# Products on GpSimd and more additions on TensorE in the last three units of an involution, shared out by a tally

## The chip, the cores and the metric

The kernel runs on one core of a Trainium2 chip. The metric is the device time in microseconds, the median of several runs. Engines are named as in the profile: PE is TensorE (PEld its weight loads), DVE is VectorE, ACT is ScalarE, POOL is GpSimd, SP issues most DMAs. A time such as "2567 us" is counted from the start of the profiled span.

## What is computed

The input `x` has 4 images of 512 channels and 64 x 64 pixels, in float32. Layer 0 is a self-attention over the 4096 pixels of each image (queries, keys and values of 128 channels), projected back to 512 channels and added to `x`. Layer 1 is a bottleneck around an involution. The change is in the involution:

```
out = relu(affine(conv1x1(x, W1), s1, b1))            # 128 channels
w = relu(affine(conv1x1(out, Wr), sr, br))            # 32 channels
w = conv1x1(w, Ws) + bs                               # 8 groups x 49 taps, for each pixel
patches = [out shifted by (i, j) for i in 7 for j in 7]
out = sum over the 49 taps of w[group, tap] * patches # 16 channels share a group's weight
x = affine(conv1x1(out, W3), s3, b3) + x
```

For each pixel and channel there are 49 products and 48 additions, and the weight of a product is one value for 16 channels.

## The kernel before

**The two jobs.** Attention goes image by image (b = 0 to 3) and within an image by chunks of 512 pixels (c = 0 to 7). It keeps TensorE busy nearly all the time. The involution of an image runs beside the attention of later chunks and the next image, on VectorE and GpSimd. It is cut into units `u` of four image rows, 16 to an image; a unit holds its pixels on the partitions (two rows of 64) and two such tiles (`NT = 2`), with the 128 channels along the free axis. `ring` is an SBUF ring of image rows, already shifted for the seven columns, which `pump` (lines 257 to 285) fills by DMA from a copy `pix` in DRAM.

**A unit** (`involution`, lines 313 to 410). `weights` (line 290) lets TensorE make all 49 x 8 weights of each pixel into a PSUM tile `pw` of 392 columns for each of the two tiles. Then come 14 to 21 steps `o` over the seven columns `x` and groups of taps `dy`, each with a product (line 371) `ring * pw` on VectorE. It covers n taps and two tiles: 1024 columns for n = 4, 768 for 3, 512 for 2, 256 for 1. The first group at x = 0 is written to `acc` directly; the others go to one of four buffers `prod` and are added to `acc` by GpSimd (line 399). When a unit has finished, its four partial sums are folded, turned so that channels lie on the partitions (`turn_unit`), and multiplied by `W3` (`close_chunk`, which makes `py` on TensorE, and `x` on VectorE at line 485, and then the store).

**The last stretch.** When the attention of the last image has been issued, `tail` becomes true (it is set behind the last call of `attention`). What is then left are the last units of image 3: unit 13, unit 14, and unit 15, the last. (Unit 12 has its products behind it there.) In the tail every second product is added by TensorE: a transposing matmul against the identity, 128 x 128 in each piece, accumulates it into the PSUM tile `pa` (line 227), which also turns it. The others go on to `acc` through GpSimd, and `add_sums` adds `acc` to `pa` at the unit's end. The rule is one line:

```python
elif tail and (o % 2 or ending and o >= len(ops) - 4):
```

`ending` means unit 15, where the order of steps also changes, so that its later taps come in pieces of 256 columns.

**Order.** Before the tail, counters (`pe`, `due`, and `free` for each engine, advanced by `takes` and `pe_us`) decide when a step is issued. In the tail nothing waits on them: the generators `finishing`, `closing` and `taps` are stepped in turn, and the tile framework and its scheduler put each engine's instructions in an order that is fixed when the program is built. Each engine takes its queue strictly in that order, and a wait at its head holds all behind it.

Of the kernel before, what the change touches and what calls it, by code (L numbers as in the profile page):

```python
# [8 lines left out]
F32 = mybir.dt.float32  # L9
# [6 lines left out]
P = 128  # L16
CT = C // P
CH = 512
# [7 lines left out]
NTAP = K * K  # L26
GC = 16
G = P // GC
# [23 lines left out]
NT = UR // 2  # L52
# [8 lines left out]
DYS = (0, 4), (4, 3)  # L61
# [12 lines left out]
HOP_US = 0.8  # L74
STEP_US = 1.0
POOL_LAG = 4.0, 7.5
PIECE = 3
TB = 32
WARM = 8
# [7 lines left out]
def fast_path(  # L87
# [20 lines left out]
    nc = tc.nc  # L108

    def pool(name, bufs, **kw):  # L110
        return ctx.enter_context(tc.tile_pool(name=name, bufs=bufs, **kw))

    const = pool("const", 1)
    xpool = pool("x", 6)
# [46 lines left out]
    pe = 0.0  # L161
    due, seen = 0.0, 0.0
    free = {"dve": 0.0, "pool": 0.0, "dma": 0.0}
    tail = []
    reds, sums_c = {}, {}
    written = {}
    landing = {}
# [7 lines left out]
    def pe_us(us):  # L175
        nonlocal pe
        pe += us

    def takes(engine, us):
        free[engine] = max(free[engine], pe) + us  # L180
# [44 lines left out]
    def turned_add(o, lhsT, start, stop):  # L225
        pe_us(0.11)
        nc.tensor.matmul(o, lhsT=lhsT, rhs=ident, start=start, stop=stop, is_transpose=True)
# [51 lines left out]
        pace()  # L279


    def weights(b, u):
        red, col = reds[b, u]
        wpools.append(wpools.pop(0))
        pw = wpools[0].tile([P, NT, CH], F32, tag="w", name=f"pw_{b}_{u}")
        for t in range(NT):

            rows = slice(t * (P // NT), t * (P // NT) + CR + 1)
            pixels = slice(col, col + P)
            mm(  # L290
                pw[:, t, : NTAP * G], red[rows, pixels], wt[rows, O_WT : O_WT + NTAP * G],
                shared=2,
            )
        return pw
# [18 lines left out]
    def involution():  # L313
        nonlocal low, due
        while True:
            while not units:
                yield "none"
            b, u = units.pop(0)
            acc = work2.tile([P, NT, 4, P], F32, tag="acc", name=f"acc_{b}_{u}")
            yield from until(free["dve"] + 0.3)  # L320
            pw = early.pop((b, u), None) or weights(b, u)
            begin = pe + 0.5
            pa, ops = None, []
            base = b * STEP + u * UR
            for dy0, n in DYS:

                at = (base + dy0) % RING
                whole = at + n + NT < RING + 1
                pieces = [(dy0, n)] if whole else [(dy0, 2), (dy0 + 2, n - 2)]
                ops += [((0, 1), x, dy, k) for x in range(K) for dy, k in pieces]  # L330
            ending = (b, u) == (B - 1, NU - 1)
            if ending:

                ops = [op for op in ops if op[2] < DYS[1][0]]
                for x in range(K):
                    ops += [((0, 1), x, 4, 1), ((0,), x, 5, 2)]
            for o, (tiles, x, dy, n) in enumerate(ops):
                if o and dy >= DYS[1][0] > ops[o - 1][2]:
                    low = base + UR
                    pump()  # L340
                    if tail and units:
                        early[units[0]] = weights(*units[0])
                rows = [(base + dy + t * 2) % RING for t in range(NT)]
                while base + dy + n + 2 * tiles[-1] > load:
                    yield "wait"
                landed = max(landing[base + dy + 2 * t + i] for t in tiles for i in range(n))
                while not tail and (
                    pe < max(begin, landed)
                    or free["dve"] > pe + (4.5 if b == B - 1 else 3.5)
                    or free["pool"] > pe + lag  # L350
                ):
                    yield "wait"
                cost = n * len(tiles) / NT
                free["pool"] = max(free["pool"], takes("dve", DVE_TAPS[0] + DVE_TAPS[1] * cost))
                takes("pool", POOL_TAPS[0] + POOL_TAPS[1] * cost)
                due -= cost
                d0 = dy - DYS[dy >= DYS[1][0]][0]
                first = x == 0 and dy < DYS[1][0]
                prod, p0 = acc, d0
                if not first:  # L360
                    prod, p0 = prods.tile(
                        [P, NT, 4, P], F32, tag="prod", name=f"prod_{b}_{u}_{o}"
                    ), 0
                nt = len(tiles)
                col = (x * K + dy) * G
                lines = ring[:, rows[0] : rows[0] + n, x, :]
                image = bass.AP(
                    tensor=lines.tensor, offset=lines.offset,
                    ap=[lines.ap[0], [(rows[1] - rows[0]) * K * P, nt], [K * P, n], [1, P]],
                )  # L370
                product = nc.vector.tensor_tensor(  # L371
                    prod[:, :nt, p0 : p0 + n, :].rearrange("p t d (g c) -> p t d g c", g=G),
                    image.rearrange("p t d (g c) -> p t d g c", g=G),
                    pw[:, :nt, col : col + n * G].unsqueeze(3)
                    .broadcast_to([P, nt, n * G, GC])
                    .rearrange("p t (d g) c -> p t d g c", d=n),
                    ALU.mult,
                )
                if not tail:
                    tc.keep_in_program_order(product)  # L380
                if first:
                    pass
                elif tail and (o % 2 or ending and o >= len(ops) - 4):

                    begun = pa is not None
                    if not begun:
                        pa = ps1.tile([P, NT, P], F32, tag=("po", "acc")[u % 2], name=f"pa_{b}_{u}")
                    closes = ending and o == len(ops) - 1
                    if closes:
                        add_sums(pa, acc, False)  # L390
                    for t in tiles:
                        for d in range(n):
                            turned_add(
                                pa[:, t, :], prod[:, t, d, :],
                                not begun and t == d == 0,
                                closes and t == tiles[-1] and d == n - 1,
                            )
                else:
                    nc.gpsimd.tensor_tensor(  # L399
                        acc[:, :nt, d0 : d0 + n, :], acc[:, :nt, d0 : d0 + n, :],  # L400
                        prod[:, :nt, :n, :], ALU.add,
                    )
                yield
            low = max(low, (b + 1) * STEP if u == NU - 1 else base + UR)
            pump()
            if pa is None:
                for n in (2, 1):
                    nc.gpsimd.tensor_tensor(  # L408
                        acc[:, :, :n, :], acc[:, :, :n, :], acc[:, :, n : 2 * n, :], ALU.add
                    )  # L410
            closing.append(turn_unit(b, u, acc, pa, takes("pool", POOL_OP * 1.5)))


    def add_sums(pa, acc, closes):
        for t in range(NT):
            for d in range(4):
                turned_add(
                    pa[:, t, :], acc[:, t, d, :], False, closes and t == NT - 1 and d == 3
                )
# [58 lines left out]
    def close_chunk(b, c, off, n, acc):  # L478
        xt = xs[b, c][:, :, off : off + n]
        yield  # L480
        for t in range(CT):
            py = ps.tile([P, CH], F32, tag="mm", name=f"py_{b}_{c}_{off}_{t}")[:, :n]
            mm(py, w_slice(O_W3, t), acc[:, off : off + n])
            takes("dve", DVE_OP * n / CH)
            nc.vector.scalar_tensor_tensor(  # L485
                xt[:, t, :], py, v1(V_S3 + t), xt[:, t, :], ALU.mult, ALU.add
            )
            if n < CH:
                nc.sync.dma_start(out_r[b, :, t, c * CH + off : c * CH + off + n], xt[:, t, :])
            for _ in range(2):  # L490
                yield
        takes("dma", X_US)
        if n == CH:
            nc.sync.dma_start(out_r[b, :, :, c * CH + off : c * CH + off + n], xt)
# [249 lines left out]
    for b in range(B):  # L744
        lag = POOL_LAG[0]
        kv = keys_values(b)
        lag = POOL_LAG[1]
        if b == 0:
# [22 lines left out]
            )  # L771
        attention(b, *kv)
    tail.append(True)
    scorepool.close()
    wpools.insert(0, pool("ps_w", 1, space=bass.MemoryType.PSUM, reuse_waits="tile"))
    wpools.reverse()
# [404 lines left out]
```

## Time and profile before

| what | us |
|---|---|
| median of 3 runs | 2601.13 (2601.11 to 2601.95) |
| the profiled execution, its own time | 2602.08 |
| its span, first to last instruction | 2600.3 |
| TensorE busy in the span | 2576.0 (99%) |
| VectorE, GpSimd, ScalarE busy in the span | 1873.2, 1828.4, 835.5 |
| chain that ended last, PE's share of the span | 89% |
| last score matmul of the attention starts | about 2530 |
| last `x` of the involution ends on VectorE | 2594.34 |

The profile's page describes one execution. For most of the span the chain that ended last runs on TensorE, in the attention. The last 70 us are different, since there is no attention left to fill TensorE with: this is the stretch that the change touches. A group row shows line, engine, operation, output and inputs with their shapes, the count, then busy time and the mean of one instruction, then the idle time of the engine ahead of it and what ended that. A chain row shows when a piece begins and how long it holds the end. The clock in the tables of stretches is the share of full speed that TensorE was granted.

### The profile page before, as it was taken

Reading aid. Unit: us, or ns where it says so; the run is one execution under the profiler, and the core shown is the slowest. Engines: PE = TensorE matmul, PEld = TensorE weight load, DVE = VectorE, ACT = ScalarE, POOL = GpSimd, SP = SyncE. Lnnn points to the kernel's source line nnn. Section 1 sums busy time; section 2 is a strip of 40 time slices with the busy share of each in tenths; the row PEclk is TensorE's granted clock in tenths of the full one; section 3 lists DMA queues with packets and bytes.
Section 4 is the critical chain, followed back from the end, with each engine's and each line's share of the span. In section 5 each row is a group of like instructions: output and inputs, shape, how many; then the busy total and the mean of one; then the engine's idle time right before and its main releaser. Section 6 shows DMA issues by size and latency. Waiting matters only on the chain.

```text
span 2600.3 us, 24194 instructions
## 1 busy us (share of the span) xinstructions
PE 2576.0 (99%) x7290; PEld 1226.7 (47%) x7290; DVE 1873.2 (72%) x2686; ACT 835.5 (32%) x1379; POOL 1828.4 (70%) x1204
## 2 busy tenths in 40 slices
PE   9999999999999999999999999999999999999997
PEld 7444444445544444444654444444464444444574
DVE  0347778877585787788676677787856677778887
ACT  1333333332233333333223333333323333333330
POOL 0006788877881788888885468887878577778986
PEclk9999999999999999999999999999999999999998
DMA  6033233445615343333651434434463432223343
GB/s 237 1 74 64 56 81 78 99 99 150 164 43 113 63 101 88 67 81 81 181 134 44 104 69 101 97 83 86 102 178 82 113 94 70 71 63 73 65 112 83
DMA packets 208472, 243.34 MB, mean 94 GB/s; under 512 B 109576, under 2 KB 128464, under 8 KB 208208
## 3 DMA queue, kind: packets, MB, share of 16 engines
q1 hardware_dynamic: 207904, 241.39, 38.5%
q8 instruction: 58, 0.95, 0.2%
q14 instruction: 78, 0.64, 0.1%
q10 hardware_dynamic: 432, 0.36, 0.1%
HBM read 192.65 MB, written 49.06 MB: 93 GB/s over the span
## 4 chain that ended last, share of the span: by engine, by line
PE 89%; POOL 5%; DVE 4%; issue 2%; ACT 0%; DVEq 0%; POOLq 0%; ACTq 0%
PE pss L223 31%; PE po L223 30%; POOL acc L399 4%; PE pv L223 4%; PE pk L223 4%; PE pq L223 4%; PE pwo L223 4%; PE p L223 4%; PE py L223 4%; DVE prod L371 2%; PE pw L223 2%; DVE pacc L734 1%; PE pr L223 1%; POOL acc L408 0%; DVE x L485 0%
## 5 line engine op out<-in xcount | busy, mean ns | idle before, releaser
L399 POOL TENSOR_TENSOR acc<-acc,prod 128x768 f32<-128x768 f32 (+3 forms) x1068 | 1704.5, 1614 | 748.8 <-DVE prod L371 704.2
L223 PE MATMUL pss<-q,k 128*128 128x512 f32 (+1 forms) x2112 | 1056.7, 585 | 0.0
L223 PE MATMUL po<-pt,v 128*128 128x512 f32 (+1 forms) x2112 | 1048.0, 581 | 0.0
L703 ACT ACTIVATE pt<-pss 128x512 f32<-128x512 f32 x1024 | 611.0, 597 | 1244.4 <-PE pss L223 1174.7
L371 DVE TENSOR_TENSOR prod<-ring,pw 128x512 f32<-128x512 f32 (+3 forms) x1099 | 887.0, 843 | 47.1 <-POOL acc L399 43.4
L734 DVE TENSOR_TENSOR pacc<-pacc,pt 128x512 f32<-128x512 f32 x958 | 665.8, 695 | 238.2 <-ACT pt L703 210.2
L223 PEld LDWEIGHTS po<-pt,v 128*128 128x128 f32 x2112 | 399.1, 190 | 481.4 <-issue 460.9
L223 PEld LDWEIGHTS pss<-q,k 128*128 128x128 f32 x2112 | 391.8, 190 | 467.2 <-issue 462.0
L431 DVE STREAM_TRANSPOSE turned<-acc 128x256 f32<-128x256 f32 x48 | 21.4, 445 | 216.0 <-POOL acc L408 216.0
L223 PE MATMUL py<-accT,wt 128*128 128x512 f32 (+1 forms) x264 | 133.8, 590 | 4.6 <-DVE x L485 3.4
L223 PE MATMUL pwo<-on,wt 128*128 128x512 f32 (+1 forms) x264 | 128.5, 579 | 0.0
L408 POOL TENSOR_TENSOR acc<-acc 128x512 f32<-128x512 f32 x122 | 121.4, 995 | 9.6
L223 PEld LDWEIGHTS pv<-wt,x 128*128 128x128 f32 x1024 | 119.6, 192 | 15.3 <-issue 15.3
L485 DVE SCALAR_TENSOR_TENSOR x<-py,vec,x 128x512 f32<-128x512 f32 (+1 forms) x132 | 96.0, 727 | 38.3 <-PE py L223 38.1
L223 PE MATMUL pv<-wt,x 128*128 128x128 f32 x1024 | 120.2, 275 | 0.0
L223 PE MATMUL p<-x,wt 128*128 128x512 f32 (+1 forms) x264 | 119.3, 580 | 0.0
L223 PE MATMUL pk<-x,wt 128*128 128x512 f32 x256 | 118.0, 600 | 0.0
L614 ACT ACTIVATE x<-x,vec 128x512 f32<-128x512 f32 (+1 forms) x132 | 92.9, 707 | 74.9 <-PE p L223 58.2
L223 PE MATMUL pq<-x,wt 128*128 128x512 f32 (+1 forms) x264 | 115.3, 579 | 0.0
L587 DVE SCALAR_TENSOR_TENSOR x<-pwo,bo,x 128x512 f32<-128x512 f32 (+1 forms) x132 | 95.3, 729 | 21.2 <-PE pwo L223 19.9
L371 DVE TENSOR_TENSOR acc<-ring,pw 128x1024 f32<-128x1024 f32 (+1 forms) x84 | 78.7, 956 | 15.6 <-PE pw L223 15.6
L223 PEld LDWEIGHTS pq<-x,wt 128*128 128x128 f32 x264 | 50.1, 190 | 59.7 <-issue 56.9
(69 smaller groups left out, 697.8 us busy)
## 6 DMA issues: line engine op xcount, KB each, us to landing
x<-x_dram SPq DMA_DIRECT2D x55, 1024.0 KB, 5.8
ring<-pix SPq DMA_DIRECT2D x74, 448.0 KB, 6.7
ring<-pix SPq DMA_DIRECT2D x24, 1344.0 KB, 9.7
out_dram<-x SPq DMA_DIRECT2D x31, 1024.0 KB, 4.5
ring<-pix SPq DMA_DIRECT2D x24, 896.0 KB, 10.4
ring<-pix SPq DMA_DIRECT2D x30, 672.0 KB, 10.9
ring<-pix SPq DMA_DIRECT2D x6, 2240.0 KB, 19.5
pix<-o1t SPq DMA_DIRECT2D x192, 32.0 KB, 1.7
```

What stands on the lines that cost most here:

```text
L223: return nc.tensor.matmul(o, lhsT=lhsT, rhs=rhs, start=start, stop=stop)
L371: product = nc.vector.tensor_tensor(prod[:, :nt, p0 : p0 + n, :].rearrange("p t d (g c) -> p t d g c", g=G), image.rearrange("p t d (g c) ...
L399: nc.gpsimd.tensor_tensor(acc[:, :nt, d0 : d0 + n, :], acc[:, :nt, d0 : d0 + n, :], prod[:, :nt, :n, :], ALU.add,)
L408: nc.gpsimd.tensor_tensor(acc[:, :, :n, :], acc[:, :, :n, :], acc[:, :, n : 2 * n, :], ALU.add)
L431: nc.vector.transpose(blocks.rearrange("p (t k q) -> p t k q", t=NT, q=TB), acc[:, :, 0, :].rearrange("p t (k q) -> p t k q", q=TB),)
L485: nc.vector.scalar_tensor_tensor(xt[:, t, :], py, v1(V_S3 + t), xt[:, t, :], ALU.mult, ALU.add)
L587: nc.vector.scalar_tensor_tensor(xt[:, t, :], pw, bo[:, t : t + 1], xt[:, t, :], ALU.add, ALU.add)
L614: nc.scalar.activation(xt[:, t, :], xt[:, t, :], AF.Identity, bias=v1(V_B3 + t))
L703: nc.scalar.activation(pt, pss, AF.Exp)
L734: nc.vector.tensor_tensor(paccs[k], paccs[k], pt, ALU.add)
```

## The change

In the tail, each step asks a new function `share` who makes the product and who adds it. There are three ways: VectorE makes it and TensorE adds it, VectorE makes it and GpSimd adds it, or GpSimd makes it and TensorE adds it. `share` keeps a tally `spent` of estimated microseconds for each of the three engines, and takes the way after which the longest tally is shortest (then the second longest, and so on). Steps that write `acc` directly, and the last six of unit 15, are always VectorE's, with TensorE adding. Other tail work (weights, sums, the `W3` matmuls and their `x`) is put on the tally with `spend`; the tally starts, when the tail starts, from what the counters `free` say is still queued on VectorE and GpSimd.

[...] when it makes its first product of a unit, `copied` has ScalarE copy `pw` there, in two instructions of 392 columns, into a buffer of the pool that holds the chunks of `x`. The products on GpSimd read this copy, and those on VectorE go on reading PSUM.

```diff
+DVE_COL, POOL_COL, PE_ADD = (0.064, 1.042e-3), (0.13, 2.19e-3), 0.115
...
+    def spend(engine, us):
+        if tail:
+            spent[engine] += us
+
+    def share(cols, adds, direct):
+
+        by = {
+            "dve": DVE_COL[0] + DVE_COL[1] * cols,
+            "pool": POOL_COL[0] + POOL_COL[1] * cols,
+            "pe": PE_ADD * cols / P,
+        }
+        ways = [("dve", "pe"), ("dve", "pool"), ("pool", "pe")]
+        if direct:
+            ways = ways[:1]
+
+        def after(way):
+            us = dict(spent)
+            us[way[0]] += by[way[0]]
+            if adds:
+                us[way[1]] += by[way[1]]
+            return us
+
+        way = min(ways, key=lambda w: sorted(after(w).values(), reverse=True))
+        spent.update(after(way))
+        return way
...
+    def copied(b, u, pw):
+        w = xpool.tile([P, CT, CH], F32, tag="x", name=f"w_{b}_{u}")
+        for t in range(NT):
+            nc.scalar.copy(w[:, t, : NTAP * G], pw[:, t, : NTAP * G])
+        return w
...
+                first = x == 0 and dy < DYS[1][0]
+                maker = adder = None
+                if tail:
+                    maker, adder = share(
+                        n * len(tiles) * P, not first, first or ending and o >= len(ops) - 6
+                    )
...
-                product = nc.vector.tensor_tensor(
+                maps = pw
+                if maker == "pool":
+                    if pw_copy is None:
+                        pw_copy = copied(b, u, pw)
+                    maps = pw_copy
+                product = (nc.gpsimd if maker == "pool" else nc.vector).tensor_tensor(
...
-                    pw[:, :nt, col : col + n * G].unsqueeze(3)
+                    maps[:, :nt, col : col + n * G].unsqueeze(3)
...
-                elif tail and (o % 2 or ending and o >= len(ops) - 4):
+                elif adder == "pe":
...
+    spent.update(pe=0.0, **{e: max(free[e] - pe, 0.0) for e in ("dve", "pool")})
```

In the built program this comes out as follows, for units 13, 14 and 15 together (instructions on GpSimd, VectorE and ScalarE; single 128 x 128 additions on TensorE):

| | before | after |
|---|---|---|
| products on VectorE (into `prod`) | 59 | 41 |
| products on GpSimd | 0 | 18 |
| additions on GpSimd | 28 | 4 |
| additions on TensorE into `pa` | 160 | 268 |
| weight copies on ScalarE | 0 | 6 |

More of the change, by code (lines that the diff above doesn't have):

```diff
@@ L164, in fast_path @@
     tail = []
+    spent = {}
     reds, sums_c = {}, {}
@@ L279, in chores @@
         pace()
+    def copied(b, u, pw):
[3 more added lines that the diff above has]
+        return w
     def weights(b, u):
         red, col = reds[b, u]
+        spend("pe", 1.06)
         wpools.append(wpools.pop(0))
@@ L322, in involution @@
             begin = pe + 0.5
+            pw_copy = None
             pa, ops = None, []
@@ L357, in involution @@
                 d0 = dy - DYS[dy >= DYS[1][0]][0]
-                first = x == 0 and dy < DYS[1][0]
                 prod, p0 = acc, d0
@@ L416, in add_sums @@
             for d in range(4):
+                spend("pe", PE_ADD)
                 turned_add(
@@ L481, in close_chunk @@
         for t in range(CT):
+            spend("pe", 0.86 * n / CH)
+            spend("dve", 0.75 * n / CH + 0.1)
             py = ps.tile([P, CH], F32, tag="mm", name=f"py_{b}_{c}_{off}_{t}")[:, :n]
```

## The prediction

> **What bounds the kernel now.** I read, in this order, the mean clock and the engines' busy time by stretches, the chain of work that ended last, the groups kept apart by shape, and the timeline of TensorE. The built order of instructions is the same in both kernels up to the third product of unit 13 (b = 3), at about 2538 us; everything that can differ lies between there and 2594.34 us, where VectorE ends its last `x`. The 5.96 us after it (last store, end of program) stay. First the stretches (span, then busy us and count of PE, PEld, DVE, ACT, POOL, the clock, DMA):
>
> ```profile
> 2538.20:2547.14 8.94, 6.97 (x47) 5.00 (x45) 8.94 (x16) 3.22 (x8) 7.46 (x5) 1.00 0.30 72
> 2554.14:2567.30 13.16, 10.79 (x48) 5.76 (x48) 12.76 (x20) 0.37 (x1) 9.45 (x7) 1.00 0.12 22
> 2567.30:2581.00 13.70, 10.37 (x41) 8.60 (x42) 11.55 (x12) 0.37 (x1) 10.16 (x5) 0.50 0.21 78
> 2581.00:2594.34 13.34, 10.09 (x47) 6.47 (x45) 8.49 (x23) 0.37 (x1) 5.99 (x6) 0.87 0.18 61
> ```
>
> VectorE is full to 2567 (12.76 of 13.16 us), GpSimd three quarters busy, ScalarE idle. After 2567.3 nobody is full, and TensorE's clock is half. The chain shows why: the end is a ladder of hand-overs.
>
> ```profile
> 2567.53 1.83 POOL acc L399
> ...
> 2571.32 1.83 POOL acc L399
> ...
> 2573.20 1.98 PE pa L227 x8
> ...
> 2581.15 2.37 POOL acc L399
> ...
> 2587.26 3.51 PE pa L227 x16
> ...
> 2593.86 0.48 DVE x L485
> ```
>
> GpSimd's additions end late, TensorE adds their sum only then, and `accT`, `py` and `x` follow. The prices (busy us, mean ns | idle before and its releaser):
>
> ```profile
> L399 POOL TENSOR_TENSOR acc<-acc,prod 128x1024 f32<-128x1024 f32 x6 | 14.2, 2364 | 4.7 <-DVE prod L371 4.5
> L371 DVE TENSOR_TENSOR prod<-ring,pw 128x1024 f32<-128x1024 f32 x11 | 12.9, 1214 | 2.1 <-PE pa L227 2.1
> L371 DVE TENSOR_TENSOR prod<-ring,pw 128x512 f32<-128x512 f32 x19 | 12.3, 680 | 0.4 <-POOL acc L399 0.3
> L399 POOL TENSOR_TENSOR acc<-acc,prod 128x256 f32<-128x256 f32 x12 | 8.7, 727 | 1.5 <-DVE prod L371 0.9
> L399 POOL TENSOR_TENSOR acc<-acc,prod 128x512 f32<-128x512 f32 x6 | 7.6, 1272 | 2.6 <-DVE prod L371 2.3
> L399 POOL TENSOR_TENSOR acc<-acc,prod 128x768 f32<-128x768 f32 x4 | 7.3, 1816 | 1.6 <-DVE prod L371 1.4
> ```
>
> And one addition on TensorE, at either clock:
>
> ```profile
> 2559.00 1.53 PE L227 MATMUL pa<-ident,prod 128*128 128x128 f32 x12
> 2576.70 1.91 PE L227 MATMUL pa<-ident,prod 128*128 128x128 f32 x8
> 2578.41 1.06 PE L223 MATMUL py<-accT,wt 128*128 128x256 f32 x2
> ```
>
> Twelve in 1.53 us, of which the last alone shows its 0.33 us latency: 0.108 us each. Eight from 2576.70 to 2578.41: 0.214 us each at half clock.
>
> [...] The rows agree for additions: (2364 - 727) / 768 = 2.13 ns. No trace here shows a GpSimd product. [...] the clock rose at 2581.0 after 2577.6 to 2581.0, nearly all transposes.
>
> **The change part by part** (units 13, 14, 15; counts from the built order).
> - Products moved to GpSimd: 7, 7 and 4. VectorE loses 4 of 1024 columns, 7 of 256, 5 of 512, 2 of 768: by mean rows 4 x 1.21 + 7 x 0.415 + 5 x 0.68 + 2 x 0.95 = 13.0 us (about 11.9 back to back). Its 2.1 us stall at 2576.5 goes too.
> - GpSimd loses 24 of 28 additions and gets 18 products. Before: 6 x 2.36 + 12 x 0.73 + 6 x 1.27 + 4 x 1.82 = 37.8 us. After, with a product at an addition's price: products 4 x 2.36 + 7 x 0.73 + 5 x 1.27 + 2 x 1.82 = 24.5, additions 1.82 + 3 x 0.73 = 4.0, sum 28.5. [...] I take equality: same operation form, two inputs of the same size.
> - TensorE: additions go from 160 to 268, so 108 x 0.108 = 11.7 us more, 23.1 at half clock.
> - ScalarE: six copies of 392 columns. The row `accT`, 256 columns, is 0.37 us and `pt`, 512 columns, 0.60, so 0.49 each, 2.9 us; between 0.4 and 0.65. ScalarE is busy 4.7 of 56 us there, but each pair is a hand-over: unit 13's waits for product 5 on VectorE, unit 14's for the second `acc` product; then product 13.7 and 14.3 on VectorE wait for the copies. Queued behind unit 13's pair are four bias steps (0.5 us each, needed only by `py` much later).
> - The copies' tile takes an `x` buffer whose store was issued long before (chunks 2 and 4): nothing waits. The third ring load now also waits for product 13.6 on GpSimd, 1.1 us later than before; the loads' data is first used past 2560, and the DMA engines were busy to about 2556: hidden by 4 us. Stores on SP's queue keep their order.
> - With four product buffers, a product on either engine waits until TensorE has added the one four before it. This is the new limit.
>
> **The walk.** I put each queue in its built order and start every instruction when its queue is free and its named waits have ended, with the durations above, 0.04 to 0.11 us per hand-over as in the chain, full clock. The same walk over the order before, with the clock it had, gives `accT` at 2547.11, 2555.31, 2575.44, 2590.90 and the end at 2594.15; the trace has 2547.14, 2555.05, 2575.26, 2590.85 and 2594.34. For the changed order:
> 1. VectorE ends product 13.5 at 2543.2 as before. Then 7.7 us of work (four `x` 1.6, checks 0.8, six 512 products 3.7, one 256 0.35, two `acc` 1.25) and 1.4 us of waits for buffers: 2552.3.
> 2. Copies 1.0, GpSimd's first product of unit 14 1.25, hand-overs 0.2: 2554.7.
> 3. TensorE now has the longest queue: 56 additions 6.05, three `py` 2.6, `pw` of unit 15 0.85, idle 0.4: 2564.6. VectorE's `acc` of 15 and product 14.18 follow: 2566.9.
> 4. GpSimd: one 768 addition 1.82, three 1024 products 7.1, one buffer wait 0.4: 2576.2.
> 5. Ladder 11.9: GpSimd addition and product to 2578.4, addition 0.7, VectorE 0.9, addition 0.7 (2580.7); meanwhile from 2580.2 VectorE does four `x` and five 256 products, 3.4 (2583.6); ten additions with latency 1.3, `accT` copy 0.4; the last `py`/`x` ladder 2.9: 2588.15.
>
> That is 6.0 us before the walked 2594.15. I take off 0.3 for GpSimd's separate wait instructions, seven or eight in the long chain at the 0.04 us or so of a hand-over: gain 5.7. The profiled execution, 2602.08 us (1.78 around the span of 2600.3), would become 2596.4. It lies 0.95 above the median 2601.13, so the median becomes 2595.4 (-0.22%).
>
> **Rivals.**
> - GpSimd product dearer (the end on the slower side). The weight operand is one value repeated 16 times; no row shows GpSimd reading that. In steps 2, 4 and 5 nothing covers it. At 1.1 times the walk ends 2589.5 (gain 4.5), at 1.2 2590.5, near 1.45 (3.4 us per 1024 columns) it equals before, at twice it ends 2606.4, 12 us late: 2613. For it: the unknown form; against: the constant cost per element.
> - TensorE becomes the bound through its clock. Between steps 3 and 4 it idles about 2 us while GpSimd makes product 15.1. [...] with the same half-clock stretches as before, 2594.3: no gain, 2601. [...]
> - The cheap product: at half price the walk ends 2585.7, gain 8.4: 2592.7.
> - The tally not shifting work is excluded by the built order, which has 18 GpSimd products.
>
> **How the numbers follow.** 0.2% (5.2 us) is about what a measurement of this kernel tells from no change. Forecast, with one short clock dip as its lower edge: 0.62 (0.54 beyond 0.2%, 0.08 within), own range 2593.5 to 2597.5. Cheap product: 0.06, faster. Clock halved for long: 0.13, within. Product 1.15 to 1.6 times: 0.09, within. Dearer than that: 0.10, slower. Faster 0.60, same 0.30, slower 0.10. The range 2592.6 to 2601.0 leaves out the dear product and the far end of the cheap one.
>
> **What would show it.** Right: GpSimd products of 1024 columns near 2.4 us; clock 1.0 through 2567 to 2588; TensorE full from 2555 to 2568; `accT` at about 2548, 2559, 2578.5, 2585; last `x` at 2588. Wrong: a product over 2.8 us, TensorE idle for GpSimd in unit 14, or a half clock past 2571.

## The result, and the profile after

| | before | changed |
|---|---|---|
| median (10 runs each) | 2599.66 us (2597.72 to 2601.95) | 2593.9 us (2591.6 to 2594.53) |
| ratio, 95% interval | | 0.9975 (0.9966 to 0.9983) |
| the profiled execution, own time | 2602.08 | 2591.92 |
| its span | 2600.3 | 2590.0 |
| the stretch (below) | 59.21 | 52.09 |

The ratio is a gain of 6.5 us, 4.4 to 8.8 by its interval; the medians lie 5.8 us apart. The two spans are 10.3 us apart, and not all of that belongs to the change. I call **the stretch** the time from the start of unit 13's 1024-column product into `acc` to the end of the last `x`, both on VectorE. It holds everything in which the two kernels differ, and it became 7.1 us shorter. The rest is in front of it (it starts at 2535.13 before and at 2532.97 after, 2.16 us) and behind it (5.96 and 4.94 us). Over all traces of this study with four product buffers that start lies between 2532.54 and 2535.13, and the piece behind between 4.94 and 5.96, with no order by kernel. So I compare stretches, and times within them counted from their start; where a time is to be laid beside the prediction's, I add 2.16 us.

The whole stretch in the view of stretches (window, length, then busy us and count of PE, PEld, DVE, ACT, POOL, the clock, DMA share, GB/s), of the kernel before:

```profile
2535.13:2594.34 59.21, 46.06 (x224) 31.26 (x224) 51.73 (x86) 4.70 (x11) 42.05 (x32) 0.86 0.32 87
```

and of the changed kernel, with three pieces of its middle:

```profile
2532.97:2585.06 52.09, 47.31 (x332) 38.06 (x332) 40.45 (x68) 7.25 (x17) 28.44 (x26) 1.00 0.37 99
...
2552.20:2566.39 14.19, 14.10 (x97) 10.80 (x97) 11.81 (x17) 1.25 (x3) 9.29 (x9) 1.00 0.11 21
2566.39:2568.07 1.68, 0.01 (x1) 0.01 (x1) 1.68 (x2) 0.00 (x0) 1.68 (x2) 1.00 0.82 316
2568.07:2574.41 6.34, 6.34 (x58) 6.34 (x59) 4.04 (x8) 0.00 (x0) 4.49 (x3) 1.00 0.23 84
```

VectorE and GpSimd lost 11.3 and 13.6 us of work. TensorE got 108 records more, 11.7 us at 0.108 us each, and is busy only 1.3 us longer. Part of that is the clock, 1.00 in place of 0.86: before, 13.3 us of TensorE's busy time lay at half clock, so by an estimate the full clock saves half of it, 6.7 us (an addition took 0.214 us at half clock and 0.108 at full). The rest fits its longer unbroken runs (56 additions took 6.33 us, 0.113 each, while before groups of four took 0.66, 0.165 each); that is argued, not tested. It is full for 14 us, stands still for 1.68 us (GpSimd makes a product; one of VectorE's lay done from 2567.1 us on, but stood behind it in TensorE's queue), and is full again. The chain that ended last, of the changed kernel (start, length, engine, tile and line), shows the same hand-over:

```profile
2552.28 4.62 PE pa L255 x39
...
2563.28 0.96 DVE prod L417
...
2564.30 0.84 POOL acc L445
...
2566.09 1.93 POOL prod L417
...
2568.07 6.35 PE pa L255 x56
...
2575.17 0.69 POOL acc L445
...
2579.74 1.88 PE pa L255 x14
```

Before, the chain at this place had three GpSimd additions in a row and one of 2.37 us later. Now the longest pieces are TensorE adding. The prices are in the groups of the stretch, kept apart by shape (busy us, mean ns | idle before and what ended it), of the changed kernel:

```profile
L255 PE MATMUL pa<-ident,prod 128*128 128x128 f32 x244 | 31.4, 275 | 2.9 <-POOL prod L417 2.1 <-DVE prod L417 0.6
...
L417 POOL TENSOR_TENSOR prod<-ring,w 128x1024 f32<-128x1024 f32 x4 | 7.7, 1930 | 5.0 <-ACT w L313 4.2 <-PE pa L255 0.9
L445 POOL TENSOR_TENSOR acc<-acc,prod 128x768 f32<-128x768 f32 x3 | 5.5, 1820 | 2.9 <-DVE prod L417 2.7
L417 POOL TENSOR_TENSOR prod<-ring,w 128x512 f32<-128x512 f32 x5 | 5.3, 1059 | 1.7 <-PE pa L255 1.2 <-ACT w L313 0.5
L417 POOL TENSOR_TENSOR prod<-ring,w 128x256 f32<-128x256 f32 x7 | 4.3, 621 | 4.2 <-PE pa L255 3.9 <-DVE prod L417 0.3
L417 POOL TENSOR_TENSOR prod<-ring,w 128x768 f32<-128x768 f32 x2 | 3.0, 1493 | 1.0 <-PE pa L255 1.0
L313 ACT COPY w<-pw 128x392 f32<-128x392 f32 x6 | 2.6, 489 | 11.5 <-DVE acc L417 10.7 <-DVE prod L417 0.8
```

A GpSimd product is not as dear as an addition, it is cheaper: 1493 ns against 1820 for 768 columns, 0.82 of it. In the last column GpSimd waits for `PE pa`, that is, for TensorE to free a product buffer (7.0 us in the four rows), and TensorE waits 2.1 us for GpSimd.

### The profile page after: what moved, and what is told of

It reads as the page before. It is cut to its first block, busy times and chain, and to the rows that moved or that the text cites. A ratio compares the mean times of both kernels' runs of the same rounds, so it can differ in the third digit from the quotient of the medians.

```text
span 2590.0 us, 24394 instructions
## 1 busy us (share of the span) xinstructions
PE 2575.1 (99%) x7398; PEld 1232.7 (48%) x7398; DVE 1861.7 (72%) x2668; ACT 838.0 (32%) x1385; POOL 1814.8 (70%) x1198
## 4 chain that ended last, share of the span: by engine, by line
PE 91%; POOL 4%; DVE 3%; issue 1%; DVEq 0%; POOLq 0%; ACT 0%; ACTq 0%
PE pss L251 32%; PE po L251 31%; PE pv L251 4%; PE pk L251 4%; PE pq L251 4%; PE py L251 4%; PE pwo L251 4%; PE p L251 4%; POOL acc L445 3%; PE pw L251 2%; DVE prod L417 1%; DVE pacc L783 1%; PE pa L255 1%; PE pr L251 1%; POOL acc L454 0%
## 5 line engine op out<-in xcount | busy, mean ns | idle before, releaser
L445 POOL TENSOR_TENSOR acc<-acc,prod 128x768 f32<-128x768 f32 (+3 forms) x1044 | 1670.7, 1618 | 740.2 <-DVE prod L417 696.8
L417 DVE TENSOR_TENSOR prod<-ring,pw 128x768 f32<-128x768 f32 (+3 forms) x1081 | 875.3, 844 | 51.2 <-POOL acc L445 45.0
## 6 DMA issues: line engine op xcount, KB each, us to landing
ring<-pix SPq DMA_DIRECT2D x30, 672.0 KB, 10.8
```

What stands on the lines that cost most here:

```text
L417: product = (nc.gpsimd if maker == "pool" else nc.vector).tensor_tensor(prod[:, :nt, p0 : p0 + n, :].rearrange("p t d (g c) -> p t d g c", ...
L445: nc.gpsimd.tensor_tensor(acc[:, :nt, d0 : d0 + n, :], acc[:, :nt, d0 : d0 + n, :], prod[:, :nt, :n, :], ALU.add,)
```

## The experiments

Ten kernels were run. This table has the stretch of each, by its trace, and the time of each against the kernel before on the same chip (a ratio under 1 is faster). The medians of different rows come from different chips and times, so the ratio is what compares them. Each stretch is that of one execution.

| kernel | stretch, us | median, us | ratio (95%) |
|---|---|---|---|
| before | 59.21 | 2599.66 | 1 |
| changed | 52.09 | 2593.9 | 0.9975 (0.9966 to 0.9983) |
| changed, GpSimd makes no products | 54.68 | 2595.9 | 0.9987 (0.998 to 0.9994) |
| changed, VectorE makes all, TensorE adds all | 54.81 | 2595.25 | 0.9981 (0.9973 to 0.9989) |
| before, zero additions everywhere | 58.27 | 2599.59 | 1.0 (0.9991 to 1.0009) |
| before, zero additions where TensorE idled | 57.10 | 2597.46 | 0.9991 (0.9982 to 0.9999) |
| changed, GpSimd products made twice | 64.24 | 2604.91 | 1.0023 (1.0015 to 1.0032) |
| before, six product buffers | 55.23 | 2594.05 | 0.9977 (0.9969 to 0.9986) |
| changed, six product buffers | 50.20 | 2588.78 | 0.9959 (0.9944 to 0.9973) |
| all on VectorE and TensorE, six buffers | 53.97 | 2592.76 | 0.997 (0.9958 to 0.9981) |
| changed, six buffers, tally at 0.108 | 49.31 | 2587.98 | 0.9954 (0.994 to 0.9967) |
| changed, other forms on GpSimd | 52.63 | (one time, 2593.64) | |

### Which part of the change brings what

The first run takes GpSimd out as a maker:

```diff
-        ways = [("dve", "pe"), ("dve", "pool"), ("pool", "pe")]
+        ways = [("dve", "pe"), ("dve", "pool")]
```

> The changed kernel, except that the tally may not choose GpSimd as maker: VectorE makes every product, TensorE or GpSimd adds, no copies. Measured by the stretch from the start of unit 13's acc product to the end of the last x on VectorE (59.2 us before, 52.1 after). Theory A (two independent parts: more additions on TensorE shorten the queues and keep the clock full, and moved products relieve VectorE on top): walked end gives a stretch of 54.7 us, about two thirds of the gain[...]. Rival B (the relief of VectorE by GpSimd products is the whole gain): stretch 57 to 60 us, VectorE busy over 95% to the last unit. Rival C (only the clock counts): stretch 52 to 53 us, as after.

```profile
2534.34:2589.02 54.68, 44.92 (x276) 32.00 (x276) 50.73 (x86) 4.70 (x11) 26.25 (x24) 1.00 0.35 94
...
L445 POOL TENSOR_TENSOR acc<-acc,prod 128x256 f32<-128x256 f32 x11 | 7.8, 726 | 13.3 <-DVE prod L417 13.3
L445 POOL TENSOR_TENSOR acc<-acc,prod 128x1024 f32<-128x1024 f32 x1 | 2.4, 2375 | 3.6 <-DVE prod L417 3.6
```

The stretch was 54.68 us, with the clock at 1.00 all through, where 54.7 was expected. So 4.5 of the 7.1 us come from giving additions to TensorE, and 2.6 from GpSimd's products. It didn't take many additions: GpSimd still made 20 of its 28 in these units. Of the eight that moved, five were of 1024 columns, at 2364 ns each on GpSimd; it kept one of six of those, and 11 of the 12 of 256 columns. The next run asks whether GpSimd is of use as an adder either:

```diff
-        ways = [("dve", "pe"), ("dve", "pool"), ("pool", "pe")]
+        ways = [("dve", "pe")]
```

> The changed kernel with one way left: VectorE makes every product, TensorE adds every one, GpSimd makes and adds nothing in the last three units (no weight copies on ScalarE). Theory A (most of the gain is from taking additions off GpSimd, whichever engine makes the products): stretch 54.3, accT at 13.2, 20.6, 37.4, 51.0 from its start, clock full; close to the run without GpSimd products (54.7), so the four additions that GpSimd kept there are worth nothing. Rival B (GpSimd's parallel work is needed for the gain; VectorE alone becomes the bound): 57 to 60.

```profile
2532.59:2587.40 54.81, 51.11 (x344) 39.50 (x344) 50.61 (x86) 4.70 (x11) 4.28 (x4) 1.00 0.35 95
```

It was 54.81 us, with `accT` at 13.14, 20.09, 37.75 and 51.32: its stretch equals that of the run before within 0.15 us. The expectation speaks of four additions that GpSimd had kept there; by the trace they were 20, and those 20 are worth nothing in the stretch. As a maker GpSimd is worth 2.7 us. The times put the changed kernel first too, but don't separate the three: the gains over the kernel before are 6.5 us (4.4 to 8.8) for it, 3.4 (1.6 to 5.2) without GpSimd's products and 4.9 (2.9 to 7.0) here, and the intervals overlap. The shares rest on the stretches.

### What the half clock had cost

To keep TensorE busy without changing what it has to deliver, the kernel before got additions of a tile of zeros to the same sum after each of its groups, first six everywhere but in unit 15's last four steps:

```diff
+WARM_ADDS = 6
...
+                    for _ in range(0 if ending and o >= len(ops) - 4 else WARM_ADDS):
+                        turned_add(pa[:, 0, :], none, False, False)
```

> The kernel before, with six additions of a zero tile put behind each group of additions on TensorE in the last stretch; they change no sum, read no product and fill only TensorE's idle time, so that its clock should stay full. Theory A: the half-clock stretch of before costs 2.7 to 3.1 us, so the stretch falls from 59.2 to about 56.3 us, clock 1.0 throughout. Rival C (the clock is most of the gain): 52 to 54 us. Rival B (the clock costs nothing, since the waits for VectorE and GpSimd set the end): 59 us or more, with the clock at 1.0.

The stretch was 58.27 us, which is none of the values expected, and the trace says why the run doesn't answer. In the view of stretches of this kernel:

```profile
2569.22:2573.22 4.00, 1.71 (x14) 1.23 (x12) 4.00 (x5) 0.25 (x1) 1.96 (x2) 1.00 0.70 262
2573.22:2577.22 4.00, 3.82 (x17) 3.60 (x18) 3.37 (x4) 0.13 (x1) 3.89 (x2) 0.57 0.02 4
2577.22:2587.22 10.00, 10.00 (x87) 9.52 (x86) 7.84 (x20) 0.00 (x0) 6.85 (x7) 1.00 0.16 53
```

The clock still fell behind a stretch in which TensorE was only 1.71 of 4.00 us busy (it waited for `acc`), and then the zeros themselves filled its queue for ten microseconds in the last unit. So I placed them anew, most of them ahead of that wait and few in the last unit:

```diff
+WARM_ADDS = (4, 5, 3)
...
+                    for _ in range(0 if ending and o >= len(ops) - 4 else WARM_ADDS[u - NU + 3] + (12 if u == NU - 2 and o > 18 else 0)):
+                        turned_add(pa[:, 0, :], none, False, False)
```

> The kernel before, plus additions of a zero tile on TensorE (4 after each group of unit 13, 5 in unit 14 with 12 more after its last two groups for TensorE, 3 in unit 15), placed where TensorE had idled, so that its clock should stay full without lengthening its queue; sums unchanged. Theory A (the half clock before cost part of the end's ladder): the walk at full clock gives a stretch of 55.6, accT at 12.0, 20.2, 40.3, 52.3. Rival B (the clock only follows from idleness and costs little): 58 to 59.5 with the clock at 1.00. If the clock falls all the same, the run says nothing and the stretch is 57 to 60.2.

The whole stretch of this kernel, and two pieces:

```profile
2532.54:2589.64 57.10, 50.78 (x345) 39.50 (x345) 51.66 (x86) 4.70 (x11) 42.21 (x32) 1.00 0.34 91
...
2556.00:2560.00 4.00, 4.00 (x29) 3.15 (x28) 4.00 (x7) 0.00 (x0) 3.42 (x3) 1.00 0.00 0
...
2568.00:2572.00 4.00, 3.23 (x28) 2.82 (x27) 4.00 (x5) 0.00 (x0) 3.54 (x2) 1.00 0.17 64
```

Now the clock was 1.00, and the stretch 2.1 us shorter than before, outside what rival B allowed, but 1.5 us longer than theory A's 55.6. The zeros have a price: in the first 23.46 us of the stretch TensorE is busy 22.53 us, where it was 19.26 before, and the third `accT` comes 41.52 us after the start, where the kernel before had 40.13 and the walk 40.3. So the half clock had cost at least 2.1 us by the stretches; the ratio puts the gain at 0.3 to 4.7 us. That it was the 3.6 of the walk is not shown.

### The buffers

The prediction called four product buffers the new limit. Two more, nothing else:

```diff
-    prods = pool("prods", 4)
+    prods = pool("prods", 6)
```

In the changed kernel:

> The changed kernel with six product buffers in place of four, nothing else. If the buffers are the new limit after the change, as the prediction says: products wait less for TensorE's additions, the stretch falls from 52.1 to about 49.6 us, and VectorE's and GpSimd's idle time put down to TensorE's additions falls from some 8 us to under 3. Rival: the queue of TensorE itself or the final ladder is the limit; then 51.5 to 52.5 us.

```profile
2531.51:2581.71 50.20, 46.71 (x332) 38.33 (x332) 40.41 (x68) 7.24 (x17) 28.14 (x26) 1.00 0.38 103
```

50.20 us, nearer to the 49.6 than to the rival: worth 1.9 us. The idle time of VectorE's and GpSimd's products put down to TensorE's additions fell from 11.5 us to 3.9, where some 8 and under 3 had been expected; GpSimd now waits 10.3 us for its weight copies, 4.7 before. In the kernel before:

> The kernel before with six product buffers in place of four; sharing unchanged. Numbers are the stretch from the start of unit 13's 1024-column product into acc to the end of the last x on VectorE (before 59.2 us, after 52.1, after with six buffers 50.2). Theory A (a product waits for the buffer four products back, in either kernel, and before those waits came from GpSimd's slow additions): the walk of the changed order gives 54.4 at full clock[...]; expected 54.4 to 57, so the kernel about 3 us faster than before. Rival B (buffers became a limit only with the change, before it was GpSimd's rate and the clock): 58.5 to 59.5, within 0.1% of before.

```profile
2531.11:2586.34 55.23, 44.54 (x224) 30.92 (x224) 51.11 (x86) 4.71 (x11) 42.09 (x32) 0.85 0.35 94
```

55.23 us, inside theory A's 54.4 to 57: worth 4.0 us, twice as much. The clock fell as before (0.85 and 0.86 over the stretch), so this gain is not the clock's. The limit isn't new. The timelines of VectorE and GpSimd in the kernel before (start, busy us, engine, line, count, idle ahead and what ended it) show it:

```profile
2571.89 4.61 DVE L371 TENSOR_TENSOR prod<-ring,pw 128x1024 f32<-128x1024 f32 x4
2578.65 3.78 DVE L371 TENSOR_TENSOR prod<-ring,pw 128x1024 f32<-128x1024 f32 x5 [2.15 <-PE pa L227]
...
2574.39 4.79 POOL L399 TENSOR_TENSOR acc<-acc,prod 128x1024 f32<-128x1024 f32 x2 [1.25 <-DVE prod L371]
2581.15 5.58 POOL L399 TENSOR_TENSOR acc<-acc,prod 128x1024 f32<-128x1024 f32 x5 [1.97 <-DVE prod L371]
```

and with six buffers:

```profile
2567.13 7.52 DVE L371 TENSOR_TENSOR prod<-ring,pw 128x1024 f32<-128x1024 f32 x8
...
2569.61 10.47 POOL L399 TENSOR_TENSOR acc<-acc,prod 128x1024 f32<-128x1024 f32 x7 [1.25 <-DVE prod L371]
```

After four products VectorE waited 2.15 us for TensorE, which had been waiting for `acc`, and behind VectorE GpSimd waited 1.97 us for its next product. With six buffers both gaps are gone and GpSimd goes through its 10.47 us in one piece. A third run asks whether buffers are short even without GpSimd: all products on VectorE, all additions on TensorE (the one way of above), six buffers.

> VectorE makes all products, TensorE adds all, GpSimd nothing in the last three units, as in the run with one way left, and six product buffers in place of four. Theory A (buffers are short only where GpSimd holds them, as adder before and as maker after): the walk gives a stretch of 54.3, accT at 13.2, 20.0, 37.4, 51.0: as with four buffers (54.8 measured). Rival B (buffers are short whoever adds, since VectorE waits for TensorE's turn): 52 to 53, and VectorE is the only bound left.

```profile
2530.86:2584.83 53.97, 50.83 (x344) 39.60 (x344) 50.36 (x86) 4.70 (x11) 4.27 (x4) 1.00 0.36 96
```

53.97 us against 54.81 with four: 0.8 us, near the walk's 54.3 and above rival B's 52 to 53. VectorE is busy 50.36 of 53.97 us, and from 2553.5 to 2578.7 us the chain that ended last runs on it; TensorE, with 50.83 us, is no less full. So two buffers are worth 4.0, 1.9 and 0.8 us in the stretch where GpSimd adds, where it makes, and where it does nothing.

All kernels with six buffers also enter the stretch earlier, at 2530.86 to 2531.51 us against 2532.54 or later with four. The buffers serve the involution before the tail too; where this 1 to 4 us comes from was not followed up.

### What a GpSimd product costs

First its place on the path. Every GpSimd product is made twice, into the same buffer from the same inputs:

```diff
-                product = (nc.gpsimd if maker == "pool" else nc.vector).tensor_tensor(
+                for _ in range(2 if maker == "pool" else 1):
+                    product = (nc.gpsimd if maker == "pool" else nc.vector).tensor_tensor(
```

> The changed kernel, with each product on GpSimd made twice into the same buffer: a product there costs about twice what it does, some 3.7 us for 1024 columns. The prediction's rival says that nothing covers a dearer product. Theory: the walk gives a stretch of 63.7 to 65.5 us, 12 us more than after and 5 more than before. Rival (GpSimd has room, being idle much of the time): under 57 us.

```profile
L418 POOL TENSOR_TENSOR prod<-ring,w 128x1024 f32<-128x1024 f32 x8 | 15.3, 1936 | 5.7 <-ACT w L313 4.2 <-PE pa L255 1.3
...
L255 PE MATMUL pa<-ident,prod 128*128 128x128 f32 x244 | 34.0, 287 | 12.1 <-POOL prod L418 10.8 <-DVE prod L418 1.3
```

GpSimd's products went from 20.3 to 40.1 us, and the stretch from 52.09 to 64.24, inside the expected range: 12.15 us for 19.8 us added, 0.61 of each. A part of that is TensorE's clock, which averaged 0.75 and 0.82 in the two pieces of 4.00 us from 2576.94 to 2584.94. TensorE waits 10.8 us for GpSimd's products where it had waited 2.1. Two products of 1024 columns, 3.87 us, lie beyond the 3.4 us at which the rival of a dearer product put its turning point, and the kernel is indeed slower than before.

Then why it is cheaper than an addition. Three things differ: it multiplies, its second input is one weight repeated 16 times, and it doesn't write over an input. In the next kernel the output is not the involution's in the last units: products of 1024 columns add the repeated weight, smaller ones multiply by as many plain columns of the copy, and additions to `acc` multiply.

```diff
+                if pooled and n < 4:
+                    product = nc.gpsimd.tensor_tensor(
+                        prod[:, :nt, p0 : p0 + n, :], image,
+                        maps[:, :nt, : n * P].rearrange("p t (d c) -> p t d c", d=n), ALU.mult,
+                    )
...
-                    ALU.mult,
+                    ALU.add if pooled else ALU.mult,
...
-                        prod[:, :nt, :n, :], ALU.add,
+                        prod[:, :nt, :n, :], ALU.mult if tail else ALU.add,
```

> The changed kernel with other forms on GpSimd in the last three units; the output is not the involution's there. GpSimd's products of 1024 columns add the repeated weight in place of multiplying it; its products of 256, 512 and 768 columns multiply by as many plain columns of the weight copy, not by 32 weights of each group repeated 16 times; its additions to acc multiply. In the changed kernel products took 1930, 1493, 1059 and 621 ns for 1024 to 256 columns, additions 1819 (768), 1272 (512), 726 (256). Theory A (the repeated operand makes the product cheaper, not the operation): 1024 columns stay near 1930, and 768, 512, 256 go to additions' 1820, 1270, 727; additions stay. Rival B (multiplying is cheaper than adding on GpSimd): 1024 columns go to 2364, the other products stay at 1493, 1059, 621, and the additions fall to 0.82 of themselves. Rival C (writing in place makes the addition slower): products stay as they are in every form.

The groups of this kernel:

```profile
L424 POOL TENSOR_TENSOR prod<-ring,w 128x1024 f32<-128x1024 f32 x4 | 7.7, 1939 | 5.0 <-ACT w L313 4.2 <-PE pa L255 0.9
...
L419 POOL TENSOR_TENSOR prod<-ring,w 128x512 f32<-128x512 f32 x5 | 6.3, 1278 | 1.1 <-PE pa L255 0.7 <-ACT w L313 0.4
L419 POOL TENSOR_TENSOR prod<-ring,w 128x256 f32<-128x256 f32 x7 | 5.1, 730 | 3.7 <-PE pa L255 3.1 <-DVE prod L424 0.3
L419 POOL TENSOR_TENSOR prod<-ring,w 128x768 f32<-128x768 f32 x2 | 3.6, 1820 | 0.5 <-PE pa L255 0.5
L452 POOL TENSOR_TENSOR acc<-acc,prod 128x256 f32<-128x256 f32 x3 | 2.2, 727 | 1.2 <-DVE prod L424 1.2
```

With plain weights the product costs what an addition costs, 1820, 1278 and 730 ns; with repeated weights the adding form costs 1939, as the product did (1930). In the last row, unit 15's three additions multiply in place and still take 727. So neither the operation nor writing in place matters: it is the repeated input. Why a repeated input is cheaper, no run shows.

### A version that beats both

With six buffers TensorE had 46.71 us of work in 50.20. The tally still counted an addition on TensorE at 0.115 us, where the trace had 0.108:

```diff
-DVE_COL, POOL_COL, PE_ADD = (0.064, 1.042e-3), (0.13, 2.19e-3), 0.115
+DVE_COL, POOL_COL, PE_ADD = (0.064, 1.042e-3), (0.13, 2.19e-3), 0.108
...
-    prods = pool("prods", 4)
+    prods = pool("prods", 6)
```

> The changed kernel with six product buffers and the tally's price of an addition on TensorE set to the 0.108 us that the trace before shows (it was 0.115). The tally then gives slightly other steps to GpSimd. Theory A (buffers and sharing are what is left): the walk gives a stretch of 48.3, accT at 13.2, 18.6, 39.7, 45.1; total 2 us below the run with six buffers alone. Rival B (TensorE is already the limit in the middle, sharing is worth nothing more): 49.7 to 50.7, equal to the run with six buffers alone.

```profile
2530.95:2580.26 49.31, 47.47 (x342) 39.49 (x342) 39.47 (x64) 7.25 (x17) 27.05 (x27) 1.00 0.39 105
```

49.31 us lies between the two expectations: sharing was worth 0.9 of the 1.9 us expected. TensorE is busy 47.47 of 49.31 us, 96%. At 2587.98 us the kernel is 0.46% (0.33 to 0.6%) faster than before. That is the fastest of the study; it is 0.8 us below the run with six buffers alone, less than what these measurements tell apart.

## Why the prediction came out right

The prediction said 2595.4 us, faster by 5.7. Measured are 2593.9, inside the forecast's own range, and a gain of 6.5 (4.4 to 8.8). The median before, 2601.13 of three runs, is 2599.66 with ten, and that alone takes 1.5 us off the time. That the medians differ by 5.8, nearly the 5.7 said, is partly luck: the stretch lost 7.1 us, where the walk had 6.0 before its deduction. Step by step, its times beside the trace of the changed kernel with 2.16 us added:

| the walk's step | predicted | trace |
|---|---|---|
| 1: VectorE through unit 14's second `acc` product | 2552.3 | 2552.3 |
| 2: GpSimd's first product of unit 14 ends | 2554.7 | 2554.4 |
| 3: TensorE through its queue; product 14.18 ends | 2564.6; 2566.9 | 2564.3; 2566.4 |
| 4: one addition, three products on GpSimd end | 2576.2 | 2574.9 |
| 5: the last `x` ends | 2588.15 | 2587.2 |

The four `accT` came at 2548.3, 2558.2, 2577.5 and 2583.9, where about 2548, 2559, 2578.5 and 2585 were said.

- **The product's price was the mis-sized term.** "I take equality" put 24.5 us for 18 products; they took 20.3. In step 4 three products of 1024 columns took 5.8 us where 7.1 were counted. A part of this was made up: the ladder of step 5 took 12.3 us, not 11.9. The walk redone with 1930, 1493, 1059 and 621 ns ends at 2587.1, a stretch of about 52.0, against 52.09 in the trace. Equality was the author's estimate, from additions, whose inputs are plain, at 2.13 ns a column. With an input repeated 16 times the trace has (1930 - 621) / 768 = 1.70 ns.
- **The 0.3 us taken off for wait instructions** isn't found: with the measured price the walk is 0.1 to 0.2 us short, all that is left for them.
- **TensorE's share.** Full from 2555 to 2568 was said; it is busy 14.10 of the 14.19 us that end at 2566.39 (2568.55 with the shift). It then stands still 1.68 us for product 15.1, as "about 2 us" said, and the clock stays at 1.00. The clock rival, which needed that pause to halve it, did not happen. That it would not was not shown beforehand: in the kernel before the clock fell to 0.50 at 2567.24, in a pause of 1.51 us behind one of 1.73 us, with TensorE busy 1.76 of the 4.00 us ahead. "TensorE idle for GpSimd in unit 14", a sign of being wrong, was seen for 0.46 us, at the place where step 2 has TensorE start behind GpSimd's product.
- **Buffers.** "This is the new limit" is half right. That it limits the changed kernel is shown by two more buffers, worth 1.9 us. "New" was wrong: they are worth 4.0 in the kernel before. The prediction had the line for it, the 2.1 us stall, and put it down as something that the change removes, not as a sign that buffers were short.
- **Copies on ScalarE.** 489 ns each were measured, 0.49 predicted. GpSimd's idle 4.2 us ahead of its first product ended with the first pair, which itself had waited for a product on VectorE. Whether GpSimd could have read `pw` itself is not shown: all 18 of its products read the copy.
- **Its sum of parts.** VectorE's 11.9 us of removed work is 11.3 in the trace, and GpSimd's 9.3 (37.8 less 28.5) is 13.6, again by the product's price. Neither is the gain. The runs say what is: 4.4 to 4.5 us from TensorE adding in place of GpSimd, where eight of the 28 suffice (the clock alone would have given at least 2.1 of it, by the run with placed zeros), and 2.6 to 2.7 from GpSimd making products.

The parts overlap. Two buffers alone give 4.0 us and TensorE's adding alone 4.4, but both together 5.2 (53.97). Both take the same wait away, which fits that overlap: VectorE's idle time ahead of its 1024-column products is 0.0 in either, 2.1 us before.

## What to carry to other kernels

At the end of a kernel, where engines hand each other work, look for the place where a maker waits for its buffer to come free. Where a slow consumer causes such a stall, here 2.15 us, try more buffers before any work is moved. When work is moved, it need not be much: eight of 28 additions, five of them of the largest size, shortened the stretch as much as all 28. A walk over the built order, with measured durations, gave the stretch to about 1 us for eight of the nine kernels whose clock it had right (the one with placed zeros was 1.5 us off), while sums of removed work did not give the gain at all. Price an operation by its form of input too: with a repeated operand the same instruction had another price, 1493 ns against 1820 for 768 columns on GpSimd.

## What was not expected of the hardware

- GpSimd's two-input operation in float32 took 1.70 ns a column with one input repeated 16 times (621 ns for 256 columns, 1930 for 1024) and 2.13 ns with both plain (730 ns for 256, 1820 for 768). At 1024 columns with the repeated input it took 1930 ns multiplying and 1939 adding.
- Under transposing matmuls alone TensorE's clock stayed up: in the changed kernel TensorE ran nothing else from 2564.25 to 2575.79 us, and the clock was 1.00 there. The prediction's own example is weaker than this one: of the time from 2577.6 to the rise at 2581.0, ordinary matmuls filled 0.85 us. Transposed tiles of zeros, between the other matmuls, did it as well: with them the kernel before ran at 1.00.
- A pause need not be long to lower the clock, nor does every pause do it. The clock fell after TensorE had been busy 1.76 of 4.00 us in the kernel before, with pauses of 1.73 and 1.51 us, and 1.71 of 4.00 in the first kernel with zeros, with a pause of 1.95 us. Around the 1.68 us pause of the changed kernel TensorE was busy 2.31 of 4.00 us (2565 to 2569), and the clock stayed at 1.00. The share of busy time doesn't tell these apart: before, the clock fell once more, at 2587.7, behind 2.41 of 4.00 us, and with GpSimd's products made twice it stayed at 1.00 behind 1.96 of 4.00 (2552.94 to 2556.94). What decides is not shown.
